# Attention: turning probabilities in 64-row halves, values in 32-column groups

## The chip, the cores and the metric

The kernel runs on one core of one Trainium2 chip. The metric is the time of one execution in microseconds (us); the median of several runs counts. In the text, PE is the matmul engine (TensorE), DVE is VectorE, ACT is ScalarE, POOL is GpSimd and SP is SyncE, which issues most DMAs. All data are float32.

## What is computed

The reference is one block of a transformer. Cut to what matters here:

```python
xn = layernorm(x)                                  # x: 4 sequences of 1024 rows, 1024 columns
q, k, v = xn @ Wq.T, xn @ Wk.T, xn @ Wv.T          # 16 query heads, 4 key/value heads of 64
att = einsum('bkgqd,bkjd->bkgqj', q, k) / 8
att = where(mask, att, -inf)                       # causal, window of 512 keys, first 4 keys always seen
y = einsum('bkgqj,bkjd->bkgqd', softmax(att), v)
s = y @ Wo.T
out = x + s * silu(ffn(xn))                        # ffn: four recurrent steps on the last row,
                                                   # broadcast through a gate to all rows
```

The change lies in the softmax probabilities and their product with the values.

## The kernel before

The kernel has three stages: normalization and projections (until about 958 us of the span), the attention loop (958 to 1876 us), and the output projection with gate and norm. The change touches the middle one.

The attention loop has 64 steps. A step takes a pair of query tiles of one sequence (128 rows each) for two groups of heads (`g`) and two heads of each (`r`, `PAIR` = 2). One tile of the pair is *far* (the 4th to 7th of the sequence): it sees 512 keys of its window, which are four key tiles, and the four first keys, the *sinks*. The other is *near* (0th to 3rd) and sees 1 to 4 key tiles, `n_near`. There are 16 steps with each number.

For each tile, these methods of `Step` are called:

- `scores` (L286 on PE): queries times keys. The contraction is 64 deep, so the two groups `g` stand in the two row halves of PE's array (written 64\*128 in the profile). DVE replaces the masked part of a far tile (L291), reduces each row to its negative maximum while copying to `pr` (L308), and ACT applies Exp with a row sum (L313, in place). The scores' PSUM tile `S` takes four banks and has one buffer.
- `normalized`: DVE takes reciprocals of the sums (L320) and multiplies the rows (L324, in place).
- `turned(k)`: PE turns the 128x128 block of key tile `k` for each `g` and `r` (L331, whole array, 128\*128) into one PSUM bank, tile `T` of pool `ps_t` with two buffers; ACT copies the bank to `pT` (L335, 512 columns). For the far tile's key 0, DVE also makes `lead` (L341), which is `pT` under a triangle mask.
- `turned_sinks`: four matmuls with the identity turn the last 32 probability columns, which hold the four sinks, for the four combinations of `g` and `r` (L353, 128\*32), into a `T` buffer; ACT copies to `sT` (L358).
- `values(k)` and `values_apart` (L363, L380): values times probabilities, summed in the PSUM tile `yp` (one buffer). Each matmul has the 64 value columns of one group as stationary operand (128\*64), so two groups stand beside each other in the array's columns.
- `stored` (L393): DVE copies `yp` out; POOL issues the DMA to `y_dram` (L398).

Between them stands the recurrent FFN as a *filler*: `filler(slot)` runs so many units of a generator that it is done two steps before the loop ends. Most units are four matmuls with 32 stationary columns (L1006, 128\*32) over a weight block that SP loads; others turn sums (L1060, 128\*128) or compute norms.

The PE order in the loop is written out by hand (`manual_schedule` for PE). The orders on DVE, ACT, POOL and SP come from the tile framework, which also places the semaphores. In the order by hand, the far and near scores of the next step stand between the turns and values of this one. A matmul of float32 has two passes, and so two records in the profile; a turn has one.

In each step, PE uses four divisions of its array: 64\*128 for scores, 128\*128 for turns, 128\*64 for values, 128\*32 for sinks and filler.

Of the kernel before, what the change touches and what calls it, by code (L numbers as in the profile page):

```python
# [8 lines left out]
F32 = mybir.dt.float32  # L9
# [6 lines left out]
P = 128  # L16
# [28 lines left out]
def recurrent_block_kernel(  # L45
# [107 lines left out]
        (b * TT + TT - 1 - t, b * TT + t) for b in range(B) for t in range(TT // 2)  # L153
    ]
    qTs, kTs, vs, biases, masks, pools = {}, {}, {}, {}, {}, {}
    sink_values, leads = {}, {}

    def load_kv(b):

# [66 lines left out]
    def attention_inputs():  # L226
        for i in PAIRED[0]:
            load_q(i)
        load_kv(0)

        make_masks()
        for name, src in (
            ("agg_b", agg_b), ("pn_gamma", pn_gamma), ("pn_beta", pn_beta),
            ("d1_b", d1_b), ("d2_b", d2_b),
        ):
            biases[name] = pools["first"].tile(list(src.shape), F32, name=f"{name}_sb")
            nc.gpsimd.dma_start(biases[name], src)

    class Step:


        def __init__(self, i, m, rp):
            self.name = f"{i}_{m}_{rp}"
            self.i, self.m, self.rp = i, m, rp
            self.b, self.t = divmod(i, TT)
            self.far = self.t >= WINDOW // P
            if self.far:
                self.cols = OWN
                self.mask = masks["far"]

                self.keys = [self.t, *range(self.t - WINDOW // P + 1, self.t)]
            else:
                self.cols = (self.t + 1) * P
                self.mask = masks["near"][:, SCOLS - self.cols :]
                self.keys = list(range(self.t + 1))
            self.pr = [
                pools["first"].tile(
                    [P, PAIR, OWN if self.far else WINDOW], F32,
                    tag="pr" if self.far else "prn", name=f"pr{self.name}_{g}", bufs=4,
                )  # L260
                for g in range(2)
            ]
            self.sums = pools["first"].tile([P, PAIR, 2], F32, tag="sums", name=f"s{self.name}", bufs=6)
            self.pT = {}

        def scores(self, rs):
# [34 lines left out]
            for r, src in zip(rs, range(len(rs))):  # L301
                for g in range(2):


                    name = f"{self.name}_{r}_{g}"
                    low = self.pr[g][:, r, :cols]
                    nm = pools["first"].tile([P, 1], F32, tag="nm", name=f"nm{name}", bufs=4)
                    nc.vector.tensor_tensor_reduce(  # L308
                        out=low, in0=S[:, src, g, :cols], in1=self.mask,
# [8 lines left out]
        def normalized(self, rs):  # L318
            rinv = pools["first"].tile([P, PAIR, 2], F32, tag="rinv", name=f"ri{self.name}_{rs[0]}", bufs=3)
            nc.vector.reciprocal(rinv[:, rs[0] : rs[-1] + 1, :], self.sums[:, rs[0] : rs[-1] + 1, :])  # L320
            for r in rs:
                for g in range(2):
                    at = self.pr[g][:, r, : self.cols]
                    nc.vector.tensor_scalar(at, at, rinv[:, r, g : g + 1], None, ALU.mult)  # L324

        def turned(self, k):

            ps = pools["ps_t"].tile([P, 2, PAIR, P], F32, tag="T", name=f"t{self.name}_{k}")
            for g in range(2):
                for r in range(PAIR):  # L330
                    nc.tensor.transpose(ps[:, g, r, :], self.pr[g][:, r, k * P : (k + 1) * P], ident)  # L331
            self.pT[k] = pools["px"].tile(
                [P, 2, PAIR * P], F32, tag="pT", name=f"pT{self.name}_{k}", bufs=4
            )
            nc.scalar.copy(self.pT[k], ps.rearrange("p g r q -> p g (r q)"))  # L335
            if self.far and k == 0:

                self.lead = pools["px"].tile(
                    [P, 2, PAIR * P], F32, tag="lead", name=f"lead{self.name}", bufs=1
                )  # L340
                nc.vector.tensor_tensor(  # L341
                    self.lead.rearrange("p g (r q) -> p (g r) q", r=PAIR),
                    self.pT[k].rearrange("p g (r q) -> p (g r) q", r=PAIR),
                    masks["lead"].unsqueeze(1).to_broadcast([P, 2 * PAIR, P]), ALU.mult,
                )

        def turned_sinks(self):

            ps = pools["ps_t"].tile([P, P], F32, tag="T", name=f"st{self.name}")
            for g in range(2):  # L350
                for r in range(PAIR):
                    at = (2 * g + r) * QUAD
                    nc.tensor.matmul(  # L353
                        ps[at : at + QUAD, :], self.pr[g][:, r, OWN - QUAD :], ident,
                        start=True, stop=True,
                    )
            self.sT = pools["first"].tile([P, P], F32, tag="sT", name=f"sT{self.name}", bufs=1)
            nc.scalar.copy(self.sT, ps)  # L358

        def added(self, pT, v, first, last):  # L360
            for g in range(2):
                cols = slice((2 * self.m + g) * HS, (2 * self.m + g + 1) * HS)
                nc.tensor.matmul(  # L363
                    self.y[g * HS : (g + 1) * HS, :], v[:, cols], pT[:, g, :],
                    start=first, stop=last,
                )

        def values(self, k):
# [6 lines left out]
        def values_apart(self):  # L375

            for r in range(PAIR):
                for g in range(2):
                    cols = slice((2 * self.m + g) * HS, (2 * self.m + g + 1) * HS)
                    nc.tensor.matmul(  # L380
                        self.y[g * HS : (g + 1) * HS, r * P : (r + 1) * P],
                        sink_values[self.b][:, r, cols], self.sT,
                        start=False, stop=False, skip_group_check=True,
                    )
# [580 lines left out]
    with ExitStack() as a:  # L965

        px = pools["px"] = a.enter_context(tc.tile_pool(name="px", bufs=1))
        pools["odd"] = a.enter_context(tc.tile_pool(name="odd", bufs=1))
        ps_t = pools["ps_t"] = a.enter_context(tc.tile_pool(name="ps_t", bufs=2, space=PSUM))
        ps_f = a.enter_context(tc.tile_pool(name="ps_f", bufs=1, space=PSUM))  # L970
        pools["ps_y"] = a.enter_context(tc.tile_pool(name="ps_y", bufs=1, space=PSUM))

# [204 lines left out]
        with tc.manual_schedule(engines={mybir.EngineType.PE}):  # L1177
            for p in range(len(order)):
# [36 lines left out]
                        load_y(0, row)  # L1215
                more = p + 1 < len(order)
                n_near = len(near.keys)
                far.turned(0)
                if more:
                    far_next, near_next = steps_of(*order[p + 1])  # L1220
                    far_next.scores((0,))
                for k in (1, 2):
                    far.turned(k)
                filler(0)
                far.turned_sinks()
                for k in range(3):
                    far.values(k)
                far.turned(3)
                if more:
                    far_next.normalized((0,))  # L1230
                    far_next.scores((1,))
                for k in range(min(2, n_near)):
                    near.turned(k)
                filler(1)
                far.values(3)
                far.values_apart()
                far.stored()
                for k in range(2, n_near):
                    near.turned(k)
                if more:  # L1240
                    far_next.normalized((1,))
                    near_next.scores(both)
                for k in range(n_near):
                    near.values(k)
                if more:
                    near_next.normalized(both)
                near.stored()
                filler(2)
                if more:
                    far, near = far_next, near_next  # L1250

# [277 lines left out]
```

## Time and profile before

| | us |
|---|---|
| median of 3 runs | 2266.17 (2265.47 to 2268.91) |
| span of the profiled execution | 2267.4 |
| attention loop within it | about 958 to 1876 |
| last stage | about 1876 to 2267 |

The profile is of one execution, whose span (first to last instruction) is 2267.4 us, 1.2 us over the median of the runs. The page lists, engine by engine, busy time, share of the span and number of instructions. Views of the trace give more: *groups* (instructions of one line, tile and shape, with mean time and idle time before them), *waits* (who waited for whom: total us, count, longest), the *list in order of time* (start, length, engine, line, tiles, shape, count; several in a row are merged), and *windows* (busy time by engine in a stretch). A form such as `128*32 128x512` is a matmul on a 128x32 division of the array with 512 streamed columns. "PEld" are the weight loads of PE. Busy times of PE come from modelled ends: a matmul is listed from its start until its result is out, so that records overlap.

### The profile page before, as it was taken

The numbers are of one execution on the slowest core, as the hardware profiler recorded it, in microseconds if no ns is written. First come the engines' busy times: TensorE is split into PE (matmuls) and PEld (weight loads), VectorE is DVE, ScalarE is ACT, GpSimd is POOL, SyncE is SP. The second block draws the span as 40 slices with busy tenths as digits, with TensorE's granted clock in tenths as the row PEclk, the third lists the DMA queues.
The fourth block names the chain that finished last, engine by engine and source line by source line (L and its number), as shares of the span: only waits on it lengthen the run. The fifth ranks groups of instructions, "written<-read, shape, count | busy, mean of one in ns | idle before, by whom it ended". The sixth has DMA issues, their size and how long they took to land. (4 is left out here: it accounts for less than half of the span.)

```text
span 2267.4 us, 34168 instructions
## 1 busy us (share of the span) xinstructions
PE 2219.1 (98%) x12614; PEld 1476.7 (65%) x12614; DVE 1707.1 (75%) x3757; ACT 903.7 (40%) x2032; POOL 383.7 (17%) x510
## 2 busy tenths in 40 slices
PE   7999999999999999999999999999999999999999
PEld 6787888888888888755555555555555554444444
DVE  5857688788778788877777777777777776777776
ACT  4343211111100000166665666566666663333332
POOL 3233234434411111400000000000000001111111
PEclk9999999999999999999999999999999999999999
DMA  8695233334632432675677776666566536765653
GB/s 284 250 358 203 72 130 128 114 120 156 248 129 96 149 130 75 192 271 190 213 219 228 229 218 209 228 208 200 180 212 230 195 89 204 197 198 161 178 166 93
DMA packets 214656, 416.61 MB, mean 184 GB/s; under 512 B 13284, under 2 KB 97332, under 8 KB 209368
## 3 DMA queue, kind: packets, MB, share of 16 engines
q1 hardware_dynamic: 170920, 266.12, 36.6%
q0 software_dynamic: 28288, 91.41, 12.9%
q10 hardware_dynamic: 15280, 56.89, 6.7%
q8 instruction: 99, 1.62, 0.3%
q14 instruction: 69, 0.57, 0.1%
HBM read 309.22 MB, written 121.93 MB: 190 GB/s over the span
## 5 line engine op out<-in xcount | busy, mean ns | idle before, releaser
L313 ACT ACTIVATE pr<-pr,nm 128x516 f32<-128x516 f32 (+4 forms) x512 | 324.5, 636 | 163.7 <-DVE nm L308 162.7
L308 DVE CUSTOM_DVE_ANT_0 pr<-S,near_mask 128x516 f32<-128x516 f32 (+4 forms) x512 | 278.3, 589 | 37.9 <-PE S L286 33.4
L335 ACT COPY pT<-t 128x512 f32<-128x512 f32 x416 | 229.6, 584 | 187.7 <-PE t L331 186.2
L286 PE MATMUL S<-kT,qT 64*128 64x512 f32 (+4 forms) x1536 | 260.2, 457 | 3.3 <-DVE nm L308 3.1
L331 PE MATMUL t<-ident,pr 128*128 128x128 f32 x1664 | 245.4, 282 | 4.8 <-ACT pT L335 2.8
L331 PEld LDWEIGHTS t<-ident,pr 128*128 128x128 f32 x1664 | 177.5, 141 | 99.7 <-issue 67.6
L363 PE MATMUL yp<-pT,v 128*64 128x256 f32 x1664 | 222.0, 391 | 0.3 <-DVE y L393 0.3
L286 PEld LDWEIGHTS S<-kT,qT 64*128 64x128 f32 x1536 | 129.7, 186 | 117.1 <-issue 95.0
L809 PE MATMUL u_g<-wg,f 128*128 128x256 f32 x864 | 197.4, 381 | 6.3 <-DVE f L762 6.3
L324 DVE TENSOR_SCALAR pr<-pr,ri 128x516 f32<-128x516 f32 (+4 forms) x512 | 198.6, 435 | 6.0
L809 PE MATMUL u_q<-f,wq_again 128*128 128x256 f32 x896 | 203.0, 379 | 0.0
L809 PEld LDWEIGHTS u_q<-f,wq_again 128*128 128x128 f32 x896 | 169.8, 190 | 23.7 <-DVE f L762 0.7
L809 PEld LDWEIGHTS u_g<-wg,f 128*128 128x128 f32 x864 | 162.8, 190 | 34.0 <-DVE f L762 11.1
L363 PEld LDWEIGHTS yp<-pT,v 128*64 128x64 f32 x1664 | 102.7, 136 | 114.3 <-issue 61.4
L1367 PE MATMUL u<-wo_sb,y 128*128 128x512 f32 x384 | 170.1, 592 | 1.1 <-DVE y L393 1.1
L398 POOL DMA_DIRECT2D y_dram<-y x64 | 36.3, 567 | 757.7 <-DVE y L393 641.4
L320 DVE RECIPROCAL ri<-s 128x2 f32<-128x2 f32 (+1 forms) x192 | 32.4, 169 | 136.2 <-ACT pr L313 135.5
L1367 PEld LDWEIGHTS u<-wo_sb,y 128*128 128x128 f32 x384 | 72.9, 190 | 92.9 <-issue 91.4
L825 DVE TENSOR_TENSOR t_q<-u_q,t_q 128x512 f32<-128x512 f32 x128 | 88.1, 688 | 54.8 <-PE u_q L809 39.1
L855 ACT COPY t_q<-u_q 128x512 f32<-128x512 f32 x28 | 16.4, 585 | 273.3 <-PE u_q L809 273.3
L825 DVE TENSOR_TENSOR t_g<-u_g,t_g 128x512 f32<-128x512 f32 x128 | 87.8, 686 | 41.1 <-PE u_g L809 36.5
L1367 PE MATMUL u<-wo_t,s 128*128 128x512 f32 x256 | 112.5, 592 | 0.0
(269 smaller groups left out, 3601.6 us busy)
## 6 DMA issues: line engine op xcount, KB each, us to landing
d_w<-in_d_w_dram SPq DMA_DIRECT2D x128, 1024.0 KB, 5.8
xT<-xT_dram SPq DMA_DIRECT2D x24, 1024.0 KB, 5.5
xn<-in_x_dram ACTq DMA_DIRECT2D x34, 512.0 KB, 5.3
xT_dram<-xT POOLq DMA_DIRECT2D x32, 512.0 KB, 6.0
qT<-q_dram SPq DMA_DIRECT2D x32, 512.0 KB, 4.5
y_dram<-y POOLq DMA_DIRECT2D x64, 256.0 KB, 3.9
y<-y_dram SPq DMA_DIRECT2D x32, 512.0 KB, 4.7
g<-g_dram SPq DMA_DIRECT2D x32, 512.0 KB, 10.6
```

Of the source, the lines that this page charges most:

```text
L286: nc.tensor.matmul(S[:, dst, g, at_s], qTs[self.i][half[g], at + r, :], k, start=True, stop=True,)
L308: nc.vector.tensor_tensor_reduce(out=low, in0=S[:, src, g, :cols], in1=self.mask, scale=-1.0 / HS**0.5, scalar=-NEG, op0=ALU.add, op1=ALU.min,
L313: nc.scalar.activation(low, low, AF.Exp, bias=nm, scale=-1.0, accum_out=self.sums[:, r, g : g + 1],)
L320: nc.vector.reciprocal(rinv[:, rs[0] : rs[-1] + 1, :], self.sums[:, rs[0] : rs[-1] + 1, :])
L324: nc.vector.tensor_scalar(at, at, rinv[:, r, g : g + 1], None, ALU.mult)
L331: nc.tensor.transpose(ps[:, g, r, :], self.pr[g][:, r, k * P : (k + 1) * P], ident)
L335: nc.scalar.copy(self.pT[k], ps.rearrange("p g r q -> p g (r q)"))
L363: nc.tensor.matmul(self.y[g * HS : (g + 1) * HS, :], v[:, cols], pT[:, g, :], start=first, stop=last,)
L398: nc.gpsimd.dma_start(y_dram[self.i][:, self.m * GROUP * P : (self.m + 1) * GROUP * P], state.pop(self.i).rearrange("p c q -> p (c q)"),)
L809: nc.tensor.matmul(bank[:, t * QD : (t + 1) * QD], stationary[:, at : at + P], moving[:, c * QD : (c + 1) * QD], start=(first and c == 0 a ...
L825: nc.vector.tensor_add(dst, in0, in1)
L1367: nc.tensor.matmul(bank, left[n][i][:, c, j * P : (j + 1) * P], wo7[i][:, c, :], start=(first and c == 0), stop=(c == KH - 1), skip_group_ ...
```

## The change

- Probabilities are turned in halves of 64 rows: each 128x128 block becomes two turns of 64 rows and 128 columns, in the two row halves of the array (64\*128), with 64 streamed columns each. The halves write two different PSUM banks.
- Two key tiles are turned together: tile `T` has two banks and one buffer (it had one bank and two buffers), and one ACT copy moves up to 1024 columns and puts the halves in place. `pT` holds a pair of key tiles, with two buffers in place of four.
- The sinks of a far tile are first put apart by POOL into one of two held 128x128 tiles (16 of its columns are written, the others stay zero), and are turned as one block, in halves.
- Values run with 32 stationary columns (128\*32), in four groups beside each other, so twice as many matmuls.
- `pr` is one tile for both groups.
- The order by hand is regrouped, so that turns stand next to scores and values next to the filler; the third filler slot now stands before the near values.

Of the four divisions of the array in the loop, 64\*128 and 128\*32 remain; the FFN's own turns (L1060) keep 128\*128.

```diff
-            self.pr = [ ... for g in range(2) ]       # [P, PAIR, columns] each, bufs=4
+            self.pr = pools["first"].tile(
+                [P, 2, PAIR, OWN if self.far else WINDOW], F32,
+                tag="pr" if self.far else "prn", name=f"pr{self.name}", bufs=2,
+            )
 def normalized(self, rs):
+            if self.far and rs[-1] + 1 == PAIR:
+                self.held = held_sinks[(PAIR * self.m + self.rp) % 2]
+                nc.gpsimd.tensor_copy(
+                    self.held.rearrange("p (g r k) -> p g r k", g=2, r=PAIR)[:, :, :, QUAD - SINK :],
+                    self.pr[:, :, :, WINDOW:],
+                )
+        def in_halves(self, ps, slot, src, n):
+            for h in range(2):
+                rows = slice(h * HS, (h + 1) * HS)
+                nc.tensor.transpose(
+                    ps[:n, h, slot * HS : (slot + 1) * HS], src[rows], ident[rows, rows]
+                )
-        def turned(self, k):
-            ps = pools["ps_t"].tile([P, 2, PAIR, P], F32, tag="T", ...)
-            for g in range(2):
-                for r in range(PAIR):
-                    nc.tensor.transpose(ps[:, g, r, :], self.pr[g][:, r, k * P : (k + 1) * P], ident)
-            nc.scalar.copy(self.pT[k], ps.rearrange("p g r q -> p g (r q)"))
+        def turned(self, *keys):
+            ps = pools["ps_t"].tile([P, 2, WIDE], F32, tag="T", ...)
+            slots = 2 * PAIR * len(keys)
+            for n, k in enumerate(keys):
+                for g in range(2):
+                    for r in range(PAIR):
+                        self.in_halves(ps, (n * 2 + g) * PAIR + r,
+                                       self.pr[:, g, r, k * P : (k + 1) * P], P)
+            pT = pools["px"].tile([P, 2, 2, PAIR * P], F32, tag="pT", ..., bufs=2)
+            nc.scalar.copy(
+                pT.rearrange("p k g c -> p (k g c)")[:, : slots * P].rearrange(
+                    "p (s h q) -> p h s q", h=2, q=HS),
+                ps[:, :, : slots * HS].rearrange("p h (s q) -> p h s q", q=HS),
+            )
 def turned_sinks(self):
-            for g in range(2):
-                for r in range(PAIR):
-                    at = (2 * g + r) * QUAD
-                    nc.tensor.matmul(ps[at : at + QUAD, :], self.pr[g][:, r, OWN - QUAD :], ident, ...)
+            self.in_halves(ps, 0, self.held, P)
+        def quads(self):
+            for at in range(0, P, QUAD):
+                g, cols = at // HS, 2 * self.m * HS + at
+                yield g, slice(at, at + QUAD), slice(cols, cols + QUAD)
 def added(self, pT, v, first, last):
-            for g in range(2):
-                cols = slice((2 * self.m + g) * HS, (2 * self.m + g + 1) * HS)
-                nc.tensor.matmul(self.y[g * HS : (g + 1) * HS, :], v[:, cols], pT[:, g, :], ...)
+            for g, rows, cols in self.quads():
+                nc.tensor.matmul(self.y[rows, :], v[:, cols], pT[:, g, :], ...)
-        ps_t = pools["ps_t"] = a.enter_context(tc.tile_pool(name="ps_t", bufs=2, space=PSUM))
+        ps_t = pools["ps_t"] = a.enter_context(tc.tile_pool(name="ps_t", bufs=1, space=PSUM))
```

The order on PE in one step, before and after (`next` is the following step, `n` is `n_near`):

```diff
-far.turned(0); far_next.scores(0); far.turned(1); far.turned(2); filler(0)
-far.turned_sinks(); far.values(0..2); far.turned(3); far_next.scores(1)
-near.turned(0); near.turned(1); filler(1)
-far.values(3); far.values_apart(); near.turned(2..n-1); near_next.scores
-near.values(0..n-1); filler(2)
+far.turned(0, 1); far_next.scores(0); filler(0)
+far.values(0..1); far.turned(2, 3); far_next.scores(1); far.turned_sinks(); filler(1)
+far.values(2..3); far.values_apart(); near.turned(0, 1); near_next.scores
+near.turned(2..n-1); filler(2); near.values(0..n-1)
```

## The prediction

> **What bounds the kernel now.** First the page: who is busy, and when. Only the attention loop (64 turns, below "steps") changes, so next its stretch alone, 958 to 1876 us.
>
> ```profile
> PE 2219.1 (98%) x12614; PEld 1476.7 (65%) x12614; DVE 1707.1 (75%) x3757; ACT 903.7 (40%) x2032; POOL 383.7 (17%) x510
> ...
> 958.00:1876.00 918.00, 904.62 (x7339) 504.65 (x7340) 682.40 (x2204) 577.57 (x1500) 51.61 (x89) 1.00 0.64 208
> ```
>
> The columns of the second line are the stretch and its length, then PE, weight loads, DVE, ACT, POOL, the clock, the DMA share and GB/s. PE is busy in 905 of 918 us. DVE has 682, 74%, so PE binds. But a PE with a quarter less to do would meet DVE. The first turn starts at 958.0 and the last copy of `yp` at 1873.5 (view by tile): I count 916 us for the loop, 14.3 a step.
>
> Then the list in order of time, for paces and mode changes:
>
> ```profile
> 968.19 0.65 PE L993 MATMUL xlT_ps<-ident,rows 4*128 4x4 f32 x8
> ...
> 1300.40 1.09 PE L331 MATMUL t<-ident,pr 128*128 128x128 f32 x8
> 1301.43 1.06 PE L1006 MATMUL d_ps<-d_w,t_cols 128*32 128x512 f32 x8
> 1302.42 0.65 PE L363 MATMUL yp<-pT,v 128*64 128x256 f32 x4
> 1302.90 0.61 PE L380 MATMUL yp<-sT,sinks 128*64 128x128 f32 x8
> ...
> 1304.46 1.56 PE L286 MATMUL S<-kT,qT 64*128 64x384 f32 x8
> 1305.95 1.51 PE L363 MATMUL yp<-pT,v 128*64 128x256 f32 x12
> ...
> 1306.07 0.56 DVE L308 CUSTOM_DVE_ANT_0 pr<-S,near_mask 128x384 f32<-128x384 f32 x1 [0.97 <-PE S L286]
> 1306.67 0.61 ACT L313 ACTIVATE pr<-pr,nm 128x384 f32<-128x384 f32 x1 [1.46 <-DVE nm L308]
> 1307.28 0.60 ACT L313 ACTIVATE pr<-pr,nm 128x384 f32<-128x384 f32 x1
> ...
> 1309.20 0.18 DVE L320 RECIPROCAL ri<-s 128x4 f32<-128x4 f32 x1 [0.47 <-ACT pr L313]
> 1309.42 1.41 DVE L324 TENSOR_SCALAR pr<-pr,ri 128x384 f32<-128x384 f32 x4
> ```
>
> A matmul's record lasts about 0.17 us past its streaming, so paces come from starts. Eight turns: 1.09 less the last one's 0.27 and the first weight load's 0.06, over 7, is 0.109 each. Of matmuls, concurrent tiles share one pass: 0.109, 0.216, 0.322, 0.429 us for 128, 256, 384, 512 columns. Four tiles of 32 columns (L1006) stream beside each other as two of 64 do.
>
> A change of division costs twice. The last turn starts at 1301.22, the next division's first matmul at 1301.43: 0.20 where 0.11 was due, **0.094 lost**. Then the first weights load with nothing to hide them: 0.10 for scores, 0.06 turns, 0.05 for 64 columns, 0.02 for 32.
>
> Last the waits: what DVE and ACT wait for even now.
>
> ```profile
> ACT pT L335 <- PE t L331: 186.2, 187, 4.1
> ACT pr L313 <- DVE nm L308: 145.5, 115, 2.4
> DVE ri L320 <- ACT pr L313: 135.5, 162, 2.4
> ```
>
> Total, count, longest. DVE's 135 us before the reciprocal are round trips over ACT. They cost nothing today, because PE is later still.
>
> **Part 1, turns in halves.** 1664 blocks took 0.109 each, 181 us. A block becomes two turns of 64 columns in two row halves that write two banks. No row shows that, so bounds: scores in the same two row halves start 0.007 apart and stream together (L286, 132 columns in 0.113), which puts 64 columns at 0.056; L993 turns from few rows, 4 columns, one behind the other: (0.65 - 0.20 - 0.02) / 7 = 0.062, its weight load bare. If the two halves' loads don't overlap, twice that: 0.124. I take **0.062**, since scores load both halves beside each other: 103 us, 78 less.
>
> A rule speaks against this. The Trainium skill, "TensorE: Matmul & The Clock Gate", section "LDWEIGHTS (loading the stationary operand)", says that a load takes columns / 1.2 ns whatever the rows: 107 ns for half a block as for a whole one, so an estimate from it leaves turning at 0.109 and the sum further down at about 2276. Here turns' loads last 141 ns and the 128-column loads of L809 190: turns load faster than the rule has it.
>
> **Part 2, sinks.** 128 passes of L353 at 0.109 (14 us) become 64 pairs at 0.062 (4): 10 less. POOL gains 64 copies of 16 elements (nearest rows: L171 copies 0.21, L112 1.06). They follow the far tile's last normalization and are needed over 5 us later, so 0; behind each in POOL's queue is a `y_dram` issue, for which three buffers wait.
>
> **Part 3, values in four groups.** Twice the matmuls, the same passes: 0, as L1006 streams four tiles in one pass. Bound above by two more starts a pass (0.007 each) on 1216 passes: 17 us. `pT` has two pairs of keys in place of four keys, and `pr` is one tile: 0, since no order of reader and writer changes with it.
>
> **Part 4, divisions.** In the order in which the instructions stand, the loop changes division 820 times before and 419 after (35 more than six a step, mostly for the FFN's own turns). At the prices above, 130 us become 61. Scores directly behind turns get a bare load of 0.05, 189 times: 10 back. **PE's sum falls by 78 + 10 + 69 - 10 = 147 us**, to about 757.
>
> **Part 5, what is late next.** The turned pair is one tile in two banks with one buffer (`ps_t` had two), and ACT empties it in one copy: 512 columns take 0.58, Exp grows 0.32 per 384 columns, so 1024 take 1.01, 1.06 with its signal. ACT is in order. For the far tile it holds copy(0,1), two Exps, copy(2,3), two Exps. `turned_sinks` needs the bank that copy(2,3) frees, that copy stands behind two Exps, and filler, values and the near scores stand behind `turned_sinks` on PE. This closes a ring through three engines. With n = 3 near key tiles, in us:
>
> - near scores until DVE starts: 1.56 (1304.46 to 1306.07, less half of the bare load)
> - first reduction 0.60 (1306.07 to 1306.67); four Exps until the reciprocal 2.53 (to 1309.20)
> - reciprocal and four normalizations 1.53; `lead` 0.60 (x64, pace of L341)
> - L291 0.46, first far reduction until Exp 0.74; two Exps, 0.715 apart, 1.43
> - copy(2,3) 1.06; sinks and filler, with one change of division, 1.05
> - values of two keys 0.86, sinks 0.44, lead 0.43, change 0.11: 1.84
> - near turns 8 x 0.062 and the bare load: 0.55
>
> Sum 13.95, against 15.3 measured between `lead` operations for n = 3. With n = 1 and 2 only scores, Exps, normalizations and near turns shrink (scores 0.70, 1.12; first reduction 0.33, 0.47; an Exp 0.385, 0.49; a normalization 0.196, 0.263): 11.2 and 12.7. With n = 4 another way is longer: ACT's order puts the copy of the second near pair behind the four near Exps, and PE waits for it: 1.98 + 0.74 + 2.82 + 1.06, values and change 0.97, next far turns 0.76, copy(0,1) 1.06, and from `lead` on as above 7.73: **17.1, longer than the 16.2 of three such steps now.** 16 steps of each kind: 16 x (11.2 + 12.7 + 13.9 + 17.1) = 878. Each of four Gelu calls takes ACT 2.9 us with its two table loads (1.28 each), now on the ring: 890. DVE's 31 weight differences (0.60) may or may not lie on it: 890 to 909, middle **899**, 17 less than 916.
>
> The profiled span, 2267.4, becomes 2250. It is 1.2 above the median of the runs, so I say **2249**.
>
> **Rivals.**
>
> 1. Forecast: halves beside each other, the ring binds: 2249, its own range 2237 to 2261.
> 2. PE stays the bound: had the ring slack, 147 us would go: 2119. For it, 682 of 757 us of DVE would fit. Against it, those 135 us of round trips on top: 817. Half of the gain would be 2193.
> 3. Slower: the halves' loads one behind the other, 0.124 a block, in `turned`. On the ring lie 4, 8, 8 and 16 blocks for n = 1 to 4: 16 x 36 x 0.062 = 36 us more, 2285. The sign turns where 17 us are used up, at 0.062 + 17 / 576 = 0.091 us per block. For it: no half turn in this trace. Against: L286 and L993.
> 4. No change: the wide copy costs more than 1.06. It is on the ring once for n up to 3, three times for n = 4: 96 copies. ACT's 1024-column rows (L1309, L1288) take 1.15 and 1.23, so up to 0.2 x 96 = 19 us: 2268.
>
> **How the numbers follow.** Forecast 50%, rival 2 10%, rival 3 25%, rival 4 15%. About 0.2%, 4.5 us, is what a measurement can tell from no change. Faster: forecast nearly whole, rival 2, a little of rival 4: 0.60. Same: 0.13. Slower: rival 3 and the rest of 4: 0.27. The range reaches from part of rival 2 to beyond rival 3: 2222 to 2290.
>
> **What would show it.** Half turns: starts of pairs 0.056 to 0.065 apart; 0.09 or more is rival 3. Changes of division: PE's mode column alternates between 64*128 and 128*32 save for FFN turns. Ring: PE idle by over 100 us in the loop, released by ACT's copies (before `st` and `yp`) and by DVE reductions (before `S`); steps with n = 4 no shorter than now. If PE still has no idle time, rival 2. If the wide copy exceeds 1.2 us, rival 4. I am wrong if the values' passes in 32-column groups exceed 0.22 us.

## The result, and the profile after

The changed kernel takes 2275.66 us (median of 5, 2269.63 to 2279.53) against 2266.22 (median of 5, 2265.47 to 2268.91): a ratio of 1.0033, interval 1.0019 to 1.0047. It is a little slower, where 17 us less were forecast. The profiled execution took 2269.63, span 2267.9, the fastest of the five.

The first line of the page and the attention loop's stretch, in the same columns as before:

```profile
PE 2110.2 (93%) x16326; PEld 1413.8 (62%) x16326; DVE 1705.1 (75%) x3757; ACT 890.3 (39%) x1840; POOL 397.8 (18%) x576
```

```profile
958.00:1876.00 918.00, 793.10 (x10998) 439.57 (x10994) 674.44 (x2195) 563.28 (x1307) 59.68 (x146) 0.98 0.65 207
```

PE has 112 us less work in the loop, and the loop is no shorter. DVE and ACT do what they did. The clock column has fallen from 1.00 to 0.98. From the first turn (954.6) to the start of the last copy of `yp` (1876.7) are 922.1 us, against 915.4 before. PE's idle time there, summed over its instructions, went from 12 to 125 us. Outside the loop the kernel became 6 us shorter.

PE's list in order of time, around one step:

```profile
1269.34 0.72 PE L339 MATMUL t<-ident,pr 64*128 64x64 f32 x16
1269.89 1.30 PE L286 MATMUL S<-kT,qT 64*128 64x512 f32 x8
...
1272.01 1.05 PE L391 MATMUL yp<-pT,v 128*32 128x256 f32 x16
...
1274.35 1.35 PE L286 MATMUL S<-kT,qT 64*128 64x512 f32 x8 [0.66 <-DVE nm L308]
1276.19 0.28 PE L339 MATMUL st<-ident,held 64*128 64x64 f32 x2 [0.48 <-ACT pT L357]
1276.40 1.06 PE L1032 MATMUL d_ps<-d_w,t_cols 128*32 128x512 f32 x8
1277.28 1.05 PE L391 MATMUL yp<-pT,v 128*32 128x256 f32 x16
```

Eight blocks turned in halves take 0.72 us where eight full turns took 1.09; their pairs start 0.061 to 0.063 apart (median 0.062; the first two of a list 0.111), the two halves of a pair 3 to 4 ns apart. Scores behind turns stay in one division. The brackets show the new waits: PE waits 0.66 for DVE's reductions, which free `S`, and 0.48 for ACT's copy, which frees the one T buffer. In the kernel before, PE's waits for those reductions were small in sum:

```profile
PE S L286 <- DVE nm L308: 3.1, 10, 0.7
```

DVE and ACT at the same place (two lists):

```profile
1270.45 0.18 DVE L320 RECIPROCAL ri<-s 128x4 f32<-128x4 f32 x1 [0.45 <-ACT pr L313]
1270.66 1.14 DVE L324 TENSOR_SCALAR pr<-pr,ri 128x256 f32<-128x256 f32 x4
1271.72 0.68 DVE L370 TENSOR_TENSOR lead<-pT,lead_keys 128x512 f32<-128x512 f32 x1
1272.32 0.42 DVE L291 COPY_PREDICATED S<-own_keys,S 128x256 f32<-128x256 uint32 x1
1272.89 0.69 DVE L308 CUSTOM_DVE_ANT_0 pr<-S,near_mask 128x516 f32<-128x516 f32 x1
...
1273.51 0.69 DVE L308 CUSTOM_DVE_ANT_0 pr<-S,near_mask 128x516 f32<-128x516 f32 x1
```

```profile
1275.06 0.99 ACT L357 COPY pT<-t 128x1024 f32<-128x1024 f32 x1
```

Read DVE's list against PE's: the scores for which DVE reduces at 1272.89 were done at about 1271.2. DVE comes to them late, because the near normalization and then `lead` stand in front. PE's next scores (1274.35) need the same `S`. This is the ring. With four near key tiles the other wait is the larger one:

```profile
1147.43 0.70 ACT L313 ACTIVATE pr<-pr,nm 128x512 f32<-128x512 f32 x1
...
1148.14 0.99 ACT L357 COPY pT<-t 128x1024 f32<-128x1024 f32 x1
...
1149.18 1.07 PE L391 MATMUL yp<-pT,v 128*32 128x256 f32 x16 [2.31 <-ACT pT L357]
```

The copy stands behind the last of four Exps, and PE stands still for 2.31 us. PE's list of waits in the changed kernel sums it up (total, count, longest):

```profile
PE S L286 <- DVE nm L308: 42.8, 48, 1.9
PE yp L391 <- ACT pT L357: 34.3, 20, 3.2
PE st L339 <- ACT pT L357: 32.7, 62, 2.1
```

### The profile page after: what moved, and what is told of

It reads as the page before. It is cut to its first block, busy times and chain, and to the rows that moved or that the text cites. A ratio compares the mean times of both kernels' runs of the same rounds, so it can differ in the third digit from the quotient of the medians.

```text
span 2267.9 us, 41563 instructions
## 1 busy us (share of the span) xinstructions
PE 2110.2 (93%) x16326; PEld 1413.8 (62%) x16326; DVE 1705.1 (75%) x3757; ACT 890.3 (39%) x1840; POOL 397.8 (18%) x576
## 3 DMA queue, kind: packets, MB, share of 16 engines
q0 software_dynamic: 28288, 91.41, 12.9%
## 4 chain that ended last, share of the span: by engine, by line
PE 59%; DVE 16%; ACT 15%; issue 6%; POOL 2%; DMA 1%; SPq 0%; ACTq 0%; DVEq 0%; POOLq 0%
PE u L1391 16%; PE u_q L835 15%; PE u_g L835 11%; ACT pr L313 10%; PE yp L391 4%; ACT pT L357 4%; DVE pr L324 3%; PE S L286 3%; DVE pr L308 3%; PE u L615 3%; PE t L339 2%; PE d_ps L1032 2%; DVE t_g L851 2%; DVE lead L370 2%; DVE S L291 1%
## 5 line engine op out<-in xcount | busy, mean ns | idle before, releaser
L286 PE MATMUL S<-kT,qT 64*128 64x512 f32 (+4 forms) x1536 | 257.7, 454 | 52.1 <-DVE nm L308 42.8
L391 PE MATMUL yp<-pT,v 128*32 128x256 f32 x3328 | 225.9, 389 | 34.4 <-ACT pT L357 34.3
L357 ACT COPY pT<-t 128x1024 f32<-128x1024 f32 (+1 forms) x224 | 210.7, 941 | 102.7 <-PE t L339 102.6
L286 PEld LDWEIGHTS S<-kT,qT 64*128 64x128 f32 x1536 | 137.3, 191 | 132.0 <-issue 96.9
L391 PEld LDWEIGHTS yp<-pT,v 128*32 128x32 f32 x3328 | 101.9, 111 | 172.6 <-issue 69.5
L339 PEld LDWEIGHTS t<-ident,pr 64*128 64x128 f32 x3328 | 123.8, 140 | 100.4 <-issue 79.7
L339 PE MATMUL t<-ident,pr 64*128 64x64 f32 x3328 | 152.3, 230 | 5.1 <-ACT pT L357 3.7
```

Of the source, the lines that this page charges most:

```text
L286: nc.tensor.matmul(S[:, dst, g, at_s], qTs[self.i][half[g], at + r, :], k, start=True, stop=True,)
L339: nc.tensor.transpose(ps[:n, h, slot * HS : (slot + 1) * HS], src[rows], ident[rows, rows])
L357: nc.scalar.copy(pT.rearrange("p k g c -> p (k g c)")[:, : slots * P].rearrange("p (s h q) -> p h s q", h=2, q=HS), ps[:, :, : slots * HS] ...
L391: nc.tensor.matmul(self.y[rows, :], v[:, cols], pT[:, g, :], start=first, stop=last,)
```

## The experiments

Four theories stood against each other, numbered as in the expectations:

- Theory 1: PE's waits for ACT's copies are on the path, and the idle time makes the clock gate halve PE's clock for a while (the granted clock in the profile is 1.00 or 0.50 at any moment).
- Theory 2: the step is a ring through DVE and ACT; PE's waits only show it, and the gate costs nothing of its own.
- Theory 3: an operation that the change touched is itself dearer.
- Theory 4: the single T buffer, which the halves force, takes back what they give.

Each kernel was timed beside the kernel before on the same chip. In the table, loop and idle are measured as above, in the profiled execution; changes are changes of division in PE's list; the clock is that of the profiled execution.

| kernel | median us | ratio to before (95%) | loop | PE idle | changes | clock |
|---|---|---|---|---|---|---|
| before | 2266.2 | | 915.4 | 12.3 | 821 | 0.997 |
| e_before_lead | 2265.48 | 1.0001 (0.9992 to 1.0010) | 913.8 | 10.8 | 821 | 0.998 |
| e_quads | 2246.47 | 0.9907 (0.9895 to 0.9920) | 895.6 | 16.1 | 670 | 0.999 |
| e_full2 | 2272.87 | 1.0027 (1.0015 to 1.0038) | 920.4 | 40.1 | 686 | 0.997 |
| e_full1 | 2308.24 | 1.0186 (1.0173 to 1.0199) | 954.4 | 71.5 | 686 | 0.996 |
| changed kernel | 2275.66 | 1.0033 (1.0019 to 1.0047) | 922.1 | 124.9 | 420 | 0.992 |
| e_after_again | 2275.62 | 1.0047 (1.0032 to 1.0063) | 933.4 | 123.4 | 420 | 0.985 |
| e_copy_first | 2260.05 | 0.9968 (0.9957 to 0.9980) | 915.8 | 111.9 | 420 | 0.988 |
| e_sinks_later | 2253.37 | 0.9936 (0.9922 to 0.9950) | 897.5 | 104.4 | 519 | 0.995 |
| e_both | 2234.25 | 0.9859 (0.9845 to 0.9873) | 886.3 | 91.1 | 519 | 0.994 |
| e_after_lead | 2238.99 | 0.9880 (0.9866 to 0.9895) | 891.4 | 97.5 | 420 | 0.992 |
| e_lead | 2196.30 | 0.9697 (0.9682 to 0.9711) | 844.1 | 58.1 | 519 | 0.998 |
| e_full2_lead | 2244.95 | 0.9909 (0.9892 to 0.9925) | 891.8 | 13.2 | 728 | 0.998 |
| e_fill | 2283.89 | 1.0072 (1.0059 to 1.0086) | 930.6 | 94.9 | 420 | 0.996 |
| e_fill2 | 2280.63 | 1.0066 (1.0053 to 1.0079) | 925.1 | 104.0 | 420 | 0.992 |

### Taking the change apart: e_quads, e_full2, e_full1

**e_quads** puts the values alone into 32-column groups, in the kernel before:

```diff
-            for g in range(2):
-                cols = slice((2 * self.m + g) * HS, (2 * self.m + g + 1) * HS)
-                nc.tensor.matmul(self.y[g * HS : (g + 1) * HS, :], v[:, cols], pT[:, g, :], ...)
+            for g, rows, cols in self.quads():
+                nc.tensor.matmul(self.y[rows, :], v[:, cols], pT[:, g, :], ...)
...                                              # values_apart in the same way
```

> The kernel before, with nothing changed but the values in 32-column groups (four passes side by side where two 64-column passes stood), full turns and the old order kept. Theory 1 (the ring of DVE, ACT and PE waits, and the clock gate that halves the clock after half-idle windows): 2266 +-3 us, a pass of 0.22 us as before, clock full in the loop. Theory 2 (the ring alone; the gate only accompanies it): the same 2266 +-3. Theory 3 (a changed operation is itself dearer): if it is the values, 2271 to 2285 and a mean per values record well over that of the kernel before.

Measured: 20 us less than before. All three theories missed it. Two lines of its list show why:

```profile
1126.46 1.06 PE L1008 MATMUL d_ps<-d_w,hid_cols 128*32 128x512 f32 x8
1127.34 0.61 PE L367 MATMUL yp<-pT,v 128*32 128x256 f32 x8
```

The filler ahead of the values is in 128*32 already. With the values in the same division they start 0.88 us after it; in the kernel before (1301.43 to 1302.42) it was 0.99. The passes cost the same, 0.22, but 151 changes of division are gone: 19.8 us of loop, 0.13 each. Where PE is the bound, as it is here with 16 us of idle time, every one counts. Theory 3 has fallen for the values.

**e_full2** and **e_full1** keep the order, the pairs, the held sinks and the values of the changed kernel, but turn whole blocks. e_full1 keeps the single T buffer of two banks and the copy of 1024 columns:

```diff
-            for h in range(2):
-                rows = slice(h * HS, (h + 1) * HS)
-                nc.tensor.transpose(
-                    ps[:n, h, slot * HS : (slot + 1) * HS], src[rows], ident[rows, rows]
-                )
+            nc.tensor.transpose(
+                ps.rearrange("p h c -> p (h c)")[:n, slot * P : (slot + 1) * P], src, ident
+            )
...                                              # the copies read the buffer in plain order
```

e_full2 has two T buffers of one bank, one per key tile, and a copy for each:

```diff
-        ps_t = ... tc.tile_pool(name="ps_t", bufs=1, space=PSUM)
+        ps_t = ... tc.tile_pool(name="ps_t", bufs=2, space=PSUM)
...
+            for k in keys:
+                ps = pools["ps_t"].tile([P, 2, PAIR, P], F32, tag="T", ...)
...
+                nc.scalar.copy(self.pT[k], ps.rearrange("p g r q -> p g (r q)"))
```

> The order of the changed kernel, its 32-column values and its held sinks, but full 128x128 turns, one T buffer of one bank per key tile, two buffers, and a copy per key tile (512 columns) as in the kernel before. It tells the single T buffer, which the halves force since two row groups need two banks, from the order. Theory 4 (the single buffer and the wide copy close the ring): PE's waits for ACT's copies all but vanish, the granted clock is back at 0.997, and PE's sum of some 835 us plus small waits sets the loop: 2200 to 2230. Theory 2 (DVE's reductions and ACT's Exps close the ring whatever the buffers): 2255 to 2300.

> The changed kernel with the half turns alone undone: same order, pairs, single T buffer and wide copy, but one 128x128 turn of 0.109 us per block where two halves took 0.062. PE gets 0.047 us for each of some 576 loop blocks in the four-key rows and fewer elsewhere, 78 us in all over the loop's blocks. Theory 1 and 2 (the ring): the turns stand in the ring once or twice a step, so 17 to 50 us come back and the rest goes into PE's idle time: 2285 to 2320, by theory 1 at a higher granted clock than the changed kernel. Theory 3 (PE's own work sets the time): 78 us more, 2354.

Measured: 2272.87 for e_full2, in theory 2's range and far from theory 4's; 2308.24 for e_full1, as theories 1 and 2 had it. With these two the way from before to after is a chain of four steps, each a part of the change:

| step | us | what it is |
|---|---|---|
| before to e_quads | -20 | values in 32-column groups |
| e_quads to e_full2 | +26 | the new order, the held sinks, `pr` as one tile |
| e_full2 to e_full1 | +35 | one T buffer, copies of two key tiles |
| e_full1 to changed | -33 | the half turns |

From e_quads to e_full2 PE's work does not change (loop less idle is 880 in both), its idle time rises by 24. The waits of e_full2 and e_full1:

```profile
PE yp L374 <- ACT pT L347: 19.3, 15, 2.2
PE S L286 <- DVE nm L308: 12.3, 18, 1.4
...
PE st L362 <- ACT pT L347: 2.1, 2, 1.7
```

```profile
PE st L337 <- ACT pT L355: 26.7, 61, 2.1
PE yp L387 <- ACT pT L355: 25.8, 16, 2.6
PE S L286 <- DVE nm L308: 12.5, 19, 1.4
```

In the first, the new order's own price is there without any half turn: the second near pair's copy behind the Exps (`yp`), and DVE late for `S`. In the second, the sinks' turn waits 26.7 us for the one buffer. So theory 4 holds for 35 us (the single buffer and the copy of two key tiles came in one step and were not told apart by a run), and falls as the whole story: with two buffers e_full2 is still 26 us slower than e_quads. Then the halves: PE's work falls from 883 to 797 us (loop less idle), 86 less, and its idle time rises by 53. The time falls by 33.

### The waits for ACT: e_copy_first, e_sinks_later, e_both

e_copy_first has the second near pair turned between the matmuls of the next near scores and their reductions. PE's order stays; on ACT the copy moves ahead of the later Exps.

```diff
-                    near_next.scores(both)
-                if n_near > 2:
-                    near.turned(*range(2, n_near))
+                    near_next.scores(both, second)   # matmuls, then second(), then the rest
...
```

> The changed kernel with the same order on PE, but ACT's copy of the second pair of near key tiles ahead of most of the next near step's four Exps. It tells how much of the near values' wait for that copy (34.3 us in the loop) is on the path. Theory 1: the wait goes, and with it most of the ten throttled stretches at 1 to 1.5 us each: 2238 to 2250 us, granted clock at or above 0.995. Theory 2: only the wait goes, half of it comes back as a later wait of the scores: 2251 to 2262, whatever the clock. Theory 3: the time lies in the passes, PE waits elsewhere as long: 2270 to 2276.

Measured: 2260.05, 16 less than the changed kernel, in theory 2's range. The wait of `yp` went from 34.3 to 8.6, but `S` waited 11 longer, nearly half of what was won, and the clock fell more often (14 throttled windows in the loop where the changed kernel's profile has 10; a throttled window is one at half clock, below):

```profile
PE S L286 <- DVE nm L311: 53.8, 51, 2.3
PE st L342 <- ACT pT L360: 31.7, 60, 2.1
...
PE yp L394 <- ACT pT L360: 8.6, 22, 1.3
```

e_sinks_later moves one call:

```diff
-                far.turned_sinks()
                 filler(1)
+                far.turned_sinks()
```

> The changed kernel with the sinks' turn behind the FFN's matmuls (about 1.07 us of PE) instead of ahead of them, so that its wait for the copy that frees the T buffer (0.5 us in each of 64 steps, 32.7 us in the loop) lies under PE work. Theory 1: 12 to 28 us less, 2248 to 2263, since PE's order makes everything behind it late by the wait and the idle time also feeds the gate. Theory 2: the ring through DVE and ACT sets the step, PE's wait only moves to the next scores: 0 to 8 less, 2268 to 2275. Theory 3: 2272 to 2279.

Measured: 2253.37, 22 less, in theory 1's range. The wait of `st` fell from 32.7 to 4.2 though 99 changes of division came back:

```profile
PE st L339 <- ACT pT L357: 4.2, 7, 1.2
```

e_both has both edits:

> The two orders of e_copy_first (-15.6 us against the changed kernel) and e_sinks_later (-22.3) together. Theory 1 (PE's waits for ACT's copies are on the path, each with the idle time it feeds to the clock gate): two different waits, so the gains add, 2232 to 2244 us. Theory 2 (the ring through DVE and ACT sets the step and PE's wait moves on to the next scores): no better than the better of the two, 2248 to 2256.

Measured: 2234.25, 41 less than the changed kernel; the two gains (16 and 22) add. So both waits for ACT are on the path, as theory 1 has it, though part of the first moves on to `S`, as theory 2 has it.

### The ring through DVE: e_after_lead, e_lead, e_before_lead, e_full2_lead

e_both still left PE idle for 91 us, mostly before `S`. e_after_lead is the changed kernel with the `lead` product moved behind the first far scores' reductions, in DVE's queue alone:

```diff
-            if self.far and 0 in keys:
-                nc.vector.tensor_tensor(self.lead, ...)          # in turned()
...
+                far.leading()                                    # the same product, pinned
                 if more:
                     far_next.normalized((0,))
                     far_next.scores((1,))
```

> The changed kernel with one DVE operation moved and nothing else: the lead product (0.69 us) stands behind the first far scores' reductions, where DVE waits for the Exps, instead of ahead of them. PE's and ACT's orders are as they were. Theory 2 (the ring closes through DVE: near normalization, lead, copy and two reductions of the first far scores, and then the second far scores, which wait for S): the wait of those scores, 52 us in the loop, shrinks by up to 0.69 in each of 64 steps: 2238 to 2262 us. Theory 1 (PE's waits for ACT's copies set it): the sinks' turn waits as much longer as the scores wait less, 2268 to 2276.

Measured: 2238.99, 37 us less with one DVE operation moved. In the two profiles, which have 10 throttled windows in the loop each, the loop is 31 us shorter (891.4 against 922.1), 0.48 of the operation's 0.60 in each of 64 steps; most of the other 6 is the lower clock of the changed kernel's other runs (0.986 to 0.989, against 0.992 and 0.993 here). Its waits:

```profile
PE yp L392 <- ACT pT L357: 34.4, 20, 3.2
PE st L339 <- ACT pT L357: 32.4, 63, 2.1
PE S L286 <- DVE nm L308: 19.3, 29, 1.9
```

Only `S` waits less (42.8 before); the other two are as they were, so the sinks' turn did not wait longer in its place. Theory 2 holds for this part.

e_before_lead makes the same move in the kernel before:

> The kernel before with the lead product moved on DVE as in e_after_lead, where it gave 37 us. Theory 2 (the place of that operation counts only because the changed kernel's step is a ring through DVE): PE is the bound here, so no change, 2263 to 2270 us. Rival (the old place costs in itself, whatever bounds the kernel): 2225 to 2250.

Measured: 2265.48, ratio 1.0001. The same edit gives nothing where PE is the bound. It is the ring that makes `lead`'s place dear.

e_lead is e_both with the same move:

> e_both (2234 us) with the lead product moved in the same way. In e_both the second far scores' wait for DVE is 68 us of 91 us of PE's idle time in the loop. Theory 2: 25 to 44 us less than e_both, 2190 to 2209. Theory 1 (what is left are waits that no DVE order changes): 2226 to 2236.

Measured: **2196.30, 3.0% faster than before** and the best of all kernels here. 79 us less than the changed kernel is the sum of the parts (41 and 37). What is left of the waits in e_both and in e_lead:

```profile
PE S L286 <- DVE nm L311: 56.7, 54, 2.3
PE yp L394 <- ACT pT L360: 9.7, 24, 1.3
```

```profile
PE S L286 <- DVE nm L311: 27.3, 37, 1.9
PE yp L395 <- ACT pT L360: 9.6, 23, 1.3
...
PE st L342 <- ACT pT L360: 4.5, 9, 1.3
```

e_full2_lead has the repaired orders of e_lead, but the full turns and two T buffers of e_full2:

> e_lead with full 128x128 turns, one T buffer per key tile, two of them, and a copy per key tile: what the half turns are worth once the orders of PE, ACT and DVE leave the ring open. Theory 2 (the halves' 0.047 us per block is real PE work, hidden in the changed kernel by the ring alone): PE's sum of about 850 us sets the loop, 2215 to 2245, and slower than e_lead by 15 to 50. Theory 4 (the single T buffer takes back what the halves give, in any order): the same as e_lead within 8.

Measured: 2244.95, 49 us slower than e_lead. Its first page line and its longest wait in the loop:

```profile
PE 2193.6 (98%) x14598; PEld 1465.5 (65%) x14598; DVE 1705.9 (76%) x3757; ACT 898.2 (40%) x2032; POOL 399.9 (18%) x576
```

```profile
PE S L286 <- DVE nm L311: 5.9, 9, 1.4
```

PE is the bound again. So the halves with their single buffer are worth 49 us once the orders leave room; in the order as changed they cost 3 (from e_full2 to the changed kernel). Theory 4 falls as a rule for any order.

### The clock gate: e_fill, e_fill2, e_after_again

The record of the granted clock shows 10 windows of 3.41 us at half clock (in 9 stretches) in the changed kernel's loop; the kernel before has one in its loop and one shortly behind it. Each stretch begins after a window in which PE's records filled 0.55 or less. Do they cost time, or do they fall on waits? e_fill and e_fill2 put matmuls of no use into the longest wait:

```diff
+                    if n_near == 4 and k == 2:
+                        near.unused(7)          # e_fill2: 4
                     near.values(k)
```

In e_fill these matmuls are marked as the start of new sums (`start=True`) in the bank in which the near values add up, and its output is not the block's; e_fill2 adds instead (`start=False`). e_fill's time is that of a kernel which leaves out part of those sums.

> The changed kernel with 28 matmuls of no use (7 rounds of four 32-column groups, 256 columns, about 1.5 us of PE) issued ahead of the second pair of near values where the near tile has four keys, so that they run inside PE's wait of 2.3 to 3 us for ACT's copy. Nothing is taken off any path. Theory 1: fewer half-idle windows, so the throttled stretches in the loop fall from ten to at most four, the granted clock rises to 0.995 or more, and the time falls by 6 to 14 us to 2262 to 2270, though work was added. Theory 2: no change to a few us slower, 2274 to 2282. Theory 3: slower by up to 24 (16 times 1.5), if PE is never truly idle there.

> As e_fill, with 4 rounds of matmuls of no use in place of 7 (two passes of 0.22 us each round, some 1.75 us, which lies inside the wait of 2.3 to 3.2 us where e_fill's 3.2 us overran it), summed into columns that nothing reads. No wait is taken away. Theory 1: the throttled stretches in the loop go from ten to four or fewer and the time falls by 5 to 12 us, to 2264 to 2271. Theory 2: the gate's stretches fall on time that PE would wait in any case, 2273 to 2279.

Both were slower than the changed kernel (2283.89 and 2280.63), above what theories 1 and 2 gave, and neither settles it. In e_fill the useless work took 3.2 us, more than the wait, so plain four-key steps grew from 17.6 to 18.1 us; there were 5 throttled windows in place of 10. In e_fill2 it fitted:

```profile
1150.03 1.91 PE L406 MATMUL yp<-v 128*32 128x256 f32 x32
1152.53 1.07 PE L391 MATMUL yp<-pT,v 128*32 128x256 f32 x16 [0.59 <-ACT pT L357]
```

The plain four-key steps kept their 17.6. But the last step of each four-key row, where that wait was 0.9 or less, grew from about 14.6 to between 15.2 and 16.2, and 7 windows in the loop were throttled still, with the waits of `S` and `st` as long as in the changed kernel (43.6 and 32.8). The fill was badly chosen: filling one wait is not filling the windows.

e_after_again is the changed kernel unchanged, for a second profile of the same instructions:

> The changed kernel once more, with nothing edited, for a second profile to lay beside the first: the same instructions with other throttled stretches. Theory 1 (the gate takes time): steps that are hit in one profile and not in the other are longer where they are hit, by 0.5 to 1.7 us per stretch of 3.41 us, and the spans differ by the difference in the number of stretches times that. Theory 2 (the stretches fall on waits): step lengths are the same whether hit or not.

Its granted clock was 0.985, its loop 933.4 us against 922.1, with 19 throttled windows where the first profile has 10. A step is counted here from one `lead` operation to the next. The 46 steps that neither profile shows throttled agree within 0.02 us. Those hit in one profile alone differ, with one exception (step 30, where 1.32 us at half clock cost nothing):

| step, near keys | first profile | second profile | throttled us, first and second |
|---|---|---|---|
| 4, n = 2 | 12.88 | 14.58 | 0 and 3.41 |
| 8, n = 3 | 14.12 | 15.72 | 0 and 3.41 |
| 11, n = 3 | 15.68 | 16.72 | 0 and 3.41 |
| 30, n = 4 | 17.62 | 17.65 | 0 and 1.32 |
| 31, n = 4 | 14.54 | 15.69 | 0 and 2.09 |
| 36, n = 2 | 15.09 | 13.40 | 3.41 and 0 |
| 41, n = 3 | 14.57 | 16.17 | 0 and 3.41 |
| 43, n = 3 | 15.68 | 17.25 | 0 and 3.41 |
| 44, n = 4 | 17.61 | 19.09 | 0 and 3.41 |

Together 11.9 us for 27.3 us at half clock, which is 8 windows: 1.5 us a window (1.0 to 1.7 in the single steps), most of the 1.7 that half the clock would take from a window full of work. By the loops, 11.3 us for 9 more windows, it is 1.3. Step 4 in the first profile, then in the second (PE's list), and the second one's stretches (columns as above; the clock is the third from the end):

```profile
1006.94 1.35 PE L286 MATMUL S<-kT,qT 64*128 64x512 f32 x8 [0.99 <-DVE nm L308]
1008.83 0.28 PE L339 MATMUL st<-ident,held 64*128 64x64 f32 x2 [0.54 <-ACT pT L357]
1009.04 1.06 PE L1032 MATMUL d_ps<-d_w,t_cols 128*32 128x512 f32 x8
1009.92 1.05 PE L391 MATMUL yp<-pT,v 128*32 128x256 f32 x16
```

```profile
1007.53 1.35 PE L286 MATMUL S<-kT,qT 64*128 64x512 f32 x8 [0.99 <-DVE nm L308]
1009.43 0.28 PE L339 MATMUL st<-ident,held 64*128 64x64 f32 x2 [0.55 <-ACT pT L357]
1009.64 1.82 PE L1032 MATMUL d_ps<-d_w,t_cols 128*32 128x512 f32 x8
1011.22 1.95 PE L391 MATMUL yp<-pT,v 128*32 128x256 f32 x16
```

```profile
1005.00:1009.80 4.80, 3.26 (x50) 1.94 (x42) 3.69 (x11) 2.47 (x6) 0.00 (x0) 1.00 0.95 355
1009.80:1013.20 3.40, 3.40 (x32) 1.36 (x28) 2.70 (x8) 1.74 (x5) 0.00 (x0) 0.50 0.25 51
1013.20:1019.60 6.40, 6.16 (x100) 3.84 (x96) 3.87 (x17) 3.99 (x10) 0.20 (x1) 1.00 0.43 159
```

Both have the same waits, 0.99 and 0.54. In the second they fell into one window, PE's records filled 0.55 of it, and the filler and values after it ran at half the clock, 1.82 for 1.06. In the first the windows were cut elsewhere, and the emptiest there was filled to 0.61. So theory 1 holds for the gate.

The Trainium skill, "TensorE: Matmul & The Clock Gate", section "What's actually happening", has a free-running window of 3413 ns and only half or full clock: these runs agree, with stretches of 3.41, 6.83, 10.24 and 13.65 us and no clock but 0.50 and 1.00. Its section "HAM oscillation — how this bites in real kernels" gives as the rule that PE should have no idle gap over about 3.4 us. Here two gaps of 0.99 and 0.55 us were enough: what stood ahead of every stretch is a window with that much idle time in sum, not one long gap, and the measurement decides.

## Why the prediction was wrong, point by point

- **What bounds the kernel.** Right: a PE with less to do meets DVE and ACT.
- **Part 1, 0.062 us per block.** Right: pairs start 0.062 apart, two halves 3 to 4 ns apart. The loads' records of 141 ns, read there as faster than 107, did not show it; the starts of the half turns do. The rule weighed there (the Trainium skill, "TensorE: Matmul & The Clock Gate", section "LDWEIGHTS (loading the stationary operand)") would, by the estimate made there, have left turning at 0.109; it does not hold for these turns.
- **Part 2.** The sinks' turn costs what was said. POOL's copies (0.20) hide.
- **Part 3, values at 0.** Right for the passes (0.22). The gain of e_quads is in part 4.
- **Part 4, 820 changes to 419.** Right in number (420 counted) and about in price: 0.13 each in e_quads, against a price of 0.094 and a bare load of 0.02 to 0.10. Of PE's 147 us, loop less idle shows 106 gone (903 to 797); some 14 of what stayed is the throttled clock (below), and some 20 are idle time that the records hide (end of this section).
- **Part 5, the ring.** Right in its terms. In the changed kernel's lists, from the `lead` at 1271.72 to the next at 1285.90, the step has 1.56, 0.60, 2.54, 1.53, 0.60, 0.57, 0.73, 1.44, 1.13, 1.09, 1.84 and 0.55: 14.18 for n = 3 against 13.95 summed. The largest miss is 0.11, behind L291. Plain steps mostly took 11.55, 12.9, 14.4 and 17.6 for n = 1 to 4, against 11.2, 12.7, 13.95 and 17.1. The long n = 4 step came as foretold. Wide copies took 0.99 to 1.01, so rival 4 is out; so are rival 3 (0.062 a block, not 0.124) and rival 2 (125 us idle).
- **What failed: the sum was made at full clock.** The prediction foresaw over 100 us of idle PE and priced it at nothing but itself. The gate halved the clock in 10 windows of the profiled loop: at 1.3 to 1.5 us each, 13 to 15 of the 23 us between the 899 forecast and 922 measured. The rest, 8 to 10, is the ring's terms, at the top of the 890 to 909 that had been given. With the 6 us of the next point the clock is about 20 of the 27 us by which the median missed; an estimate without them, 2256, would still be faster than before. The trace before had a sign of it: its one throttled window in the loop, from 1210.9, follows a window filled to 0.29.
- **The profiled execution was the least throttled.** The other four had granted clocks of 0.986 to 0.989 against 0.992, and took 6 to 10 us more. The median misses the forecast by 27, to about 1 us of rounding: 23 in the loop, less 6 outside it, 6 for the other runs' lower clock, and 3 because the forecast was put 1.2 under a span, while an execution takes 1.7 longer than its span.

Of the theories, 3 has fallen, and 4 is left with the 35 us of the single buffer in this order; the step is the ring of theory 2, and theory 1 is right for the two waits on ACT and for the gate. The change does what it says, PE's work falls by over 100 us, and all of it went into three waits (`S` on DVE, `yp` and `st` on ACT) and the gate's price for them. The first two waits appear with the new order, in e_full2 already, the third with the single buffer, in e_full1.

Where the 27 us are that loop less idle does not show as gone, after the clock's share: a record lasts some 0.16 us past its streaming, so each wait looks that much too short. The rows bear it out. Scores that follow half turns without a wait start 0.059 behind the last one; where they wait (63 times), 0.223 passes before any idle time is listed. For the 15 waits of `yp` behind values it is 0.379, against a pass of 0.22, and for the 62 waits of `st` 0.273, against the 0.112 that a pass of 132 columns takes. That makes some 22 us in these 140 waits; the kernel before has 32 waits in all, and some 3 us of it.

What stays open are the last 5 to 8 of the 147, and which of e_lead's last waits (27 us before `S`) can be moved, which was not tried.

## What to carry to other kernels

When a change takes work from the bound engine, walk the order of the next two engines' queues before counting the gain: here one 0.6 us DVE operation ahead of the reductions that free PSUM cost 37 us with the clock's share, and moving three things (a copy ahead of Exps, a turn behind filler, that product) turned 0.3% slower into 3.0% faster. Take a change apart into a chain of single edits; the part with no gain of its own in the plan (32-column values) gave 20 us alone, by keeping neighbours in one division. And do not sum a step with idle PE at full clock.

## What the runs showed of the hardware

- PE's clock falls to half for whole windows of 3.41 us after a window filled to 0.55 or less, even by gaps under 1 us each; one such window costs 1.3 to 1.5 us in the mean. No fuller window began a stretch in any loop here, though some of 0.42 to 0.55 began none. In e_sinks_later one stretch lasted 13.65 us, four windows.
- The windows do not start with the program: the first throttled one began at 83.6 us in one profile of the changed kernel and at 84.8 in the other. The same kernel's runs differ, 0.985 to 0.992 granted and 2269.63 to 2281.05 us, in step with each other.
- Two 64-row half turns in two banks run beside each other (3 to 4 ns apart), and a block costs 0.062 us in place of 0.109.
- A change of division with its first weight load costs 0.13 us on a PE that is the bound (19.8 us for 151).
